# Four layers on one core: the last batch's normalisation by ScalarE in two passes, and the last pair's products evicted by VectorE

## The chip, the cores and the metric

The kernel runs on one core of a Trainium2 chip. A time is the device time of one execution in microseconds (us). The kernel before was timed in three executions, and one more was taken with the hardware profiler. Times in the text that look like "at 906.20" are microseconds from the start of the profiled span.

The engines are named as the profile names them: PE (TensorE) multiplies matrices, DVE is VectorE, ACT is ScalarE, POOL is GpSimd, SP is SyncE, which issues most DMAs. Each engine works through its own list of instructions in order.

## The reference, cut to what matters

Four sublayers follow one another on eight batches of 512 tokens by 256 features, each with a residual and a layernorm. The last is a mixture of experts, and the change lies behind it:

```python
dispatch, combine = ...            # top 2 of 8 experts, capacity 160, in 2 groups of 2048 tokens
expert_in = jnp.einsum('gtec,gth->egch', dispatch, x)
h = jax.nn.relu(jnp.einsum('egch,ehf->egcf', expert_in, wi))
expert_out = jnp.einsum('egcf,efh->egch', h, wo)
y = jnp.einsum('gtec,egch->gth', combine, expert_out)
...
x = _layernorm(x + y, axis=-1)     # (x - mean) / sqrt(var + 1e-5) over the 256 features
```

## The kernel before, in words

Each batch is a tile of 128 partitions by `NC` = 4 chunks of 256 features. The sixteen steps (group, expert) are taken in an order in which the last pair of experts of group 1 are steps 14 and 15. An expert's two matrix products (`expert_in`, `expert_out`) leave its output in `eoT`. `combine(i)` turns three column blocks per pair back by PE into PSUM, multiplies each row by its gate while evicting it to a tile `eo`, and adds it to the rows of `y_d` in DRAM by an indirect DMA. `y_d` already holds the residual.

The last pair (`last`, steps 14 and 15) is not added in DRAM. Its three `eo` blocks stay on the chip, and the rest of the kernel runs on two tracks:

- `finish(b)` for the batches 4 to 7 of group 1 begins when the additions of step 13 have landed. It loads the batch from `y_d` into a tile `z` (SP), runs `layernorm`, and stores `z` to `out` (SP). `layernorm(..., on_act=True)` takes per chunk `bn_stats` and `bn_aggr` on DVE (lines 360, 361), then one small DVE instruction for variance + eps (`rsqrt`, tile `ln_rs`), one POOL instruction for the power -1/2 (also `ln_rs`), one small DVE instruction for the shift (`ln_nb`), and four ACT instructions that normalise a chunk each, with a per-partition scale and bias.
- `fetch`, `sums` and `finish_last` treat the rows that the last pair touches. `fetch` gathers them from `y_d` (`tail_y`), `sums` adds up on PE what the last pair brings each row (line 1674; the block of step 14 first, the two of step 15 after it, into three PSUM banks), and `finish_last` adds this on DVE, normalises three blocks, and scatters them into `out` with three indirect DMAs from POOL (`put`, line 1702). These rows must overwrite what the batches' stores wrote, so the first scatter waits for all stores of `out`.

The order of the instructions on each engine comes from a planner in the file. `op(engine, cost, t, fn, ...)` looks for the first free slot of its engine at or after the planned time `t`, books it there, and queues the call. `flush` issues the calls in order of planned time. An instruction that is planned earlier is therefore ahead of a later one on its engine, whatever the chip does. Instructions on `DVS` and `POOL` also book a shared slot list, "port". The stages are Python generators, and `interleave` resumes the one whose time comes first; a stage that resumes early books its slots before the others.

Due times set the order here. All four `finish` stages begin at one planned time, which is called T here, and queue their loads in the order 4, 5, 6, 7. They resume at the `landing` that the plan supposes, and book their whole layernorm at that moment:

```python
landing = t + (9.0 if g == 0 else 4.0 + 2.9 * (b - B // G))   # T + 4.0, 6.9, 9.8, 12.7
```

`tail["stored"]` is the planned time at which the stores have landed; `finish_last` books its scatters from there.

Of the kernel before, what the change touches and what calls it, by code (L numbers as in the profile page):

```python
# [11 lines left out]
F32 = mybir.dt.float32  # L12
F32R = mybir.dt.float32r
I32 = mybir.dt.int32
AF = mybir.ActivationFunctionType
ALU = mybir.AluOpType
# [4 lines left out]
P = 128  # L21
B, S, D = 8, 512, 256
NC = S // P
# [5 lines left out]
G = 2  # L29
# [9 lines left out]
LN_EPS = 1e-5  # L39
# [42 lines left out]
def tile_layers(ctx: ExitStack, tc: tile.TileContext, ins, out, at):  # L82
# [52 lines left out]
    ACT, DVE, POOL, SP, GELU, EXP, DVS, POOLD = range(8)  # L135
# [5 lines left out]
    V, A, GP, T = nc.vector, nc.scalar, nc.gpsimd, nc.tensor  # L141
# [3 lines left out]
    XB, TB, EX, B8 = 4, 3, 3, 2  # L145
    EW = 3

    class Plan:
        now = 0.0
        slow = 0.0  # L150
        t = 0.0
# [14 lines left out]
    def give(tag, t, n=1):  # L166
        Plan.free[tag] += [t] * n

    def take(tag, n=1):

        times = sorted(Plan.free[tag])
        assert len(times) >= n, tag
        Plan.free[tag] = times[n:]
        return times[n - 1]

    def op(engine, cost, t, fn, *args, use=None, drop=None, bank=None, **kw):


        if engine in (GELU, EXP):
            cost += 0.0 if engine == Plan.loaded else TABLE  # L180
            engine, Plan.loaded = ACT, engine
        users = [engine]
        if engine in (DVS, POOL):
            users.append("port")
        engine = users[0] = {DVS: DVE, POOLD: POOL}.get(engine, engine)
        t = t + HOP
        if use is not None:
            t = max(t, take(use) + HOP)
        if engine != SP:
            length = max(cost - OVERLAP[engine], 0.05)  # L190
            found = False
            while not found:
                found = True
                for user in users:
                    for a, b in Plan.busy[user]:
                        if t + length <= a:
                            break
                        if b > t:
                            t, found = b, False
            for user in users:  # L200
                bisect.insort(Plan.busy[user], (t, t + length))
                while Plan.busy[user][0][1] < Plan.t - 30.0:
                    Plan.busy[user].pop(0)
        Plan.count += 1
        heapq.heappush(Plan.events, (t, Plan.count, lambda: fn(*args, **kw)))  # L205
        t += cost
        if drop is not None:
            give(drop, t)
        if bank is not None:
            release(bank, t)  # L210
        return t
# [5 lines left out]
    def pe(cost):  # L217


        start = max(Plan.now, Plan.t)  # L220
        if start - Plan.now > 1.5:
            Plan.slow = start + (1.5 if start - Plan.now < 3.0 else 8.0)
        cost += min(max(Plan.slow - start, 0.0) / 2, cost)
        Plan.now = Plan.t = start + cost
        return Plan.now + PE_OUT
# [9 lines left out]
    def release(ps, t):  # L235
        Plan.banks[Plan.bank_of.pop(id(ps))[1]] = t

    def need(t, n=1):

        while True:  # L240
            r = max(t + HOP_PE, sorted(Plan.banks)[n - 1] + HOP if n else 0.0)
            yield "pe", r if r < HELD else Plan.t + 0.5
            if not n or sorted(Plan.banks)[n - 1] <= Plan.t + 1e-6:
                return
# [7 lines left out]
    def later(t):  # L252

        return "other", t
# [58 lines left out]
    def power(n):  # L313
        return {1: 0.56, 2: 0.7}.get(n, 1.02)

    def rsqrt(dst, src, scale, eps, t, bank=None):

        t = op(
            DVE if bank else DVS, 0.17, t, V.tensor_scalar, dst, src, scale, eps, ALU.mult, ALU.add,
            bank=bank,  # L320
        )
        return op(
            POOL, power(dst.shape[-1]), t,
            GP.tensor_tensor, dst, dst, mhalf.to_broadcast(list(dst.shape)), ALU.pow,
        )
# [26 lines left out]
    def layernorm(pool, dst, src, ts, on_act=False):  # L352


        st = pool.tile([P, NC, 6], F32, tag="ln_st", bufs=2, name="ln_st")
        mv = pool.tile([P, NC, 2], F32, tag="ln_mv", bufs=2, name="ln_mv")
        rs = pool.tile([P, NC], F32, tag="ln_rs", bufs=2, name="ln_rs")

        def stats(c):
            nc.vector.bn_stats(st[:, c, :], src[:, c, :])  # L360
            nc.vector.bn_aggr(mv[:, c, :], st[:, c, :])  # L361

        for c in range(NC):
            t = op(DVE, 0.61, ts[c], stats, c, use="ln" if c == 0 else None)
        ready = t = rsqrt(rs, mv[:, :, 1], 1.0, LN_EPS, t)
        if on_act:
            nb = pool.tile([P, NC], F32, tag="ln_nb", bufs=2, name="ln_nb")
            t = op(
                DVS, 0.16, t, V.scalar_tensor_tensor, nb, mv[:, :, 0], -1.0, rs, ALU.mult, ALU.mult
            )  # L370
        ends = []
        for c in range(NC):
            if on_act:
                e = op(
                    ACT, 0.58, t, A.activation, dst[:, c, :], src[:, c, :], AF.Identity,
                    bias=nb[:, c : c + 1], scale=rs[:, c : c + 1],
                )
            else:
                e = op(
                    DVS, 0.41, t, V.tensor_scalar, dst[:, c, :], src[:, c, :], mv[:, c, 0:1],  # L380
                    rs[:, c : c + 1], ALU.subtract, ALU.mult,
                )
            ends.append(e)
        give("ln", e)
        return mv, rs, ready, ends

    srcs, gates, logits = {}, {}, {}
# [181 lines left out]
    with ExitStack() as stages:  # L569
# [5 lines left out]
        wk = stages.enter_context(tc.tile_pool(name="wk", bufs=1))  # L575
# [869 lines left out]
        pools = {}  # L1445
# [131 lines left out]
        tail, stored = {}, []  # L1577

        def combine(i):


            g, e = order[i]
            last = i >= len(order) - 2
            pair, half = divmod(e, 2)
            n_in = added[g, pair]
            for j in ((0, 1), (1, 2))[half]:
                n_in[j] += 1
            for j, n in enumerate(COLS):
                if n_in[j] != (1, 2, 1)[j]:
                    continue  # L1590
                n_in[j] = -9
                col = pair * 3 + j
                yield from need(0.0)
                ps = bank("eo_tp")
                for m in range(NK):
                    T.transpose(  # L1596
                        ps[:n, m * P : (m + 1) * P], eoT[g, pair][:, m, j * P : j * P + n], ident
                    )
                eo = wk.tile([P, D], F32, tag="scm", bufs=SCM, name=f"eo_{g}_{col}")
                t = op(  # L1600
                    ACT, 0.47, pe(0.24), A.activation, eo[:n], ps[:n, :D], AF.Copy,
                    scale=gates[g][:n, col : col + 1], bank=ps, use="scm",
                )
                if last:
                    tail[j], done = eo, t
                    continue
                done = op(
                    POOLD, 1.87, max(t, Plan.landed), GP.indirect_dma_start,
                    out=y_d[g], in_=eo[:n], in_offset=None, compute_op=ALU.add,
                    out_offset=bass.IndirectOffsetOnAxis(ap=srcs[g][:n, col : col + 1], axis=0),  # L1610
                )
                Plan.landed = done + 2.9
                give("scm", Plan.landed)
            if max(n_in) < 0:
                give("xsT", Plan.now)
                give("eoT", Plan.now)
            yield later(done)
            return done + (0.0 if last else 2.9)
# [63 lines left out]
        def finish_last():  # L1682
# [46 lines left out]
            yield later(t)  # L1729
            return t + 3.0  # L1730

        def finish(b):

            g = b * G // B
            z = wk.tile([P, NC, D], F32, tag="x", bufs=XB, name=f"z_{b}")
            t = Plan.t
            dma(t, z, rows_of(y_d, b))
            landing = t + (9.0 if g == 0 else 4.0 + 2.9 * (b - B // G))
            yield later(landing)
            e = max(layernorm(wk, z, z, [landing] * NC, on_act=(g == 1))[3])  # L1740

            def store():
                stored.append(
                    nc.sync.dma_start(out=out[b].rearrange("(c p) d -> p c d", p=P), in_=z)
                )

            op(SP, 0.0, e, store)
            tail["stored"] = max(tail.get("stored", 0.0), e + 2.5)
            give("x", e + 4.0)
            yield later(e + 4.0)  # L1750
            return e + 2.5
# [4 lines left out]
        n = len(order)  # L1756
# [105 lines left out]
```

## Time and profile before

| What | Value |
|---|---|
| device time, median of 3 (range) | 930.57 us (930.12 to 933.92) |
| device time of the profiled execution | 931.42 us |
| its span | 929.6 us, 18769 instructions |
| mean granted PE clock | 0.982 |
| busy PE / DVE / ACT / POOL | 881.7 / 607.9 / 453.0 / 397.2 us |
| loads of the batches 4 to 7, issued | 896.8 to 898.6 |
| stores of these batches, issued | 906.7, 909.9, 913.1, 916.3 |
| three last scatters, begun on POOL | 919.98, 921.33, 923.66 |

Over nearly the whole span PE is busy. The rows below concern the last 35 us only: from the start of the `finish` loads to the end. In a timeline row the columns are start, duration, engine, line, operation, out<-in, shapes, count, and in brackets the idle time of the engine before it with what ended it. Line 205 is the planner's call, so that tiles and not lines tell the operations apart.

### The profile page before, as it was taken

To read this page: it belongs to the slowest core of one execution; us is meant where nothing else is said; L and a number is where in the kernel's file an instruction comes from. 1 tells how busy PE (TensorE), PEld (TensorE's weight loads), DVE (VectorE), ACT (ScalarE), POOL (GpSimd) and SP (SyncE) were. 2 spreads that over 40 slices of the span, in tenths; PEclk is the share of its full clock that TensorE was granted. 3 is DMA by queue.
4 is the path that set the end of the run, shared out by engine and by line. 5 is a ranking of instruction groups with operands and counts; after the bars stand their busy time and mean duration, and the time that the engine had idled before them with its cause. 6 is when DMAs were issued, how large, how long until landed. Compare 5 with 4: busy or idle time off the path is not lost. (4 is left out here: it accounts for less than half of the span.)

```text
span 929.6 us, 18769 instructions
## 1 busy us (share of the span) xinstructions
PE 881.7 (95%) x7628; PEld 687.9 (74%) x7628; DVE 607.9 (65%) x1530; ACT 453.0 (49%) x866; POOL 397.2 (43%) x404
## 2 busy tenths in 40 slices
PE   7899999999999999999999999999999999999892
PEld 4777777777767677677767676786787889999781
DVE  3945367669777847877887778578678654621223
ACT  2327356537652684486287535838536343122223
POOL 2425542744453263445434542732653332362233
PEclk9999999999999999999999999999999999999795
DMA  7030000001000100010020001050143356168742
GB/s 212 12 114 1 1 2 1 2 24 46 2 1 24 47 2 2 23 47 1 1 69 2 1 2 46 2 182 1 46 126 115 108 185 196 24 191 290 241 116 105
DMA packets 49894, 60.69 MB, mean 65 GB/s; under 512 B 5680, under 2 KB 44784, under 8 KB 49808
## 3 DMA queue, kind: packets, MB, share of 16 engines
q1 hardware_dynamic: 45952, 53.92, 17.4%
q0 software_dynamic: 3856, 5.57, 3.1%
q8 instruction: 60, 0.98, 0.4%
q14 instruction: 26, 0.21, 0.1%
HBM read 43.76 MB, written 15.73 MB: 64 GB/s over the span
## 5 line engine op out<-in xcount | busy, mean ns | idle before, releaser
L1167 PE MATMUL pr_ps<-prT,fT 128*128 128x257 f32 x512 | 117.4, 381 | 0.2 <-DVE f_ss L205 0.2
L1167 PEld LDWEIGHTS pr_ps<-prT,fT 128*128 128x128 f32 x512 | 95.2, 190 | 14.7 <-DVE f_ss L205 0.5
L205 POOL TENSOR_TENSOR fsq<-fsq,fsf 128x512 f32<-128x512 f32 x56 | 72.2, 1288 | 37.5 <-ACT fsf L205 35.3
L1530 PE MATMUL wi_ps<-xsT,wi 128*128 128x160 f32 x512 | 78.2, 308 | 0.1
L1559 PE MATMUL wo_ps<-e_hT,wo 128*128 128x160 f32 x512 | 74.5, 301 | 0.0
L1530 PEld LDWEIGHTS wi_ps<-xsT,wi 128*128 128x128 f32 x512 | 73.3, 196 | 1.3 <-ACT xsT L205 0.6
L205 DVE TENSOR_TENSOR hm<-hs,cst 128x512 f32<-128x512 f32 x96 | 60.2, 675 | 19.6 <-PE hs L1306 19.1
L1559 PEld LDWEIGHTS wo_ps<-e_hT,wo 128*128 128x128 f32 x512 | 70.8, 190 | 1.8 <-issue 1.5
L205 DVE TENSOR_TENSOR scm<-sc,cst 128x512 f32<-128x512 f32 x96 | 60.8, 679 | 15.4 <-PE sc L955 15.4
L205 ACT ACTIVATE e_hT<-wi_ps 128x480 f32<-128x480 f32 (+1 forms) x48 | 25.3, 526 | 87.4 <-PE wi_ps L1530 87.4
L205 POOL TENSOR_TENSOR ln_rs<-ln_rs,mhalf 128x4 f32<-128x4 f32 x32 | 33.3, 1040 | 80.7 <-DVE ln_rs L205 80.7
L205 POOL DMA_INDIRECT y_d<-eo,srci x21 | 32.8, 1561 | 71.4 <-ACT eo L205 35.7
L205 POOL TENSOR_TENSOR scm<-scm,cst 128x512 f32<-128x512 f32 x32 | 41.2, 1289 | 49.7 <-ACT scm L205 49.7
L205 DVE STREAM_TRANSPOSE hT<-pad 128x512 f32<-128x512 f32 x64 | 59.3, 959 | 3.5 <-ACT pad L205 3.0
L905 PE MATMUL qk_ps<-xT,wqkv 128*128 128x512 f32 x128 | 60.6, 617 | 1.0 <-ACT xT L205 1.0
L1247 PE MATMUL qk_ps<-l1T,x2T 128*128 128x512 f32 x128 | 61.5, 603 | 0.0
L205 POOL TENSOR_TENSOR hm<-hm,cst 128x512 f32<-128x512 f32 x32 | 41.1, 1284 | 33.5 <-ACT hm L205 33.5
L1138 PE MATMUL fc_ps<-x1T_l,fcT 128*128 128x512 f32 x128 | 53.8, 420 | 0.6 <-DVE x1T_l L205 0.5
L205 POOL TENSOR_SCALAR pad<-pad,lamv 128x128 f32<-128x128 f32 x32 | 12.0, 374 | 97.9 <-DVE pad L205 97.9
L1138 PE MATMUL fc_ps<-x1T_h,fcT 128*128 128x512 f32 x128 | 50.2, 392 | 0.0
L205 ACT ACTIVATE x<-x,ln_nb,ln_rs 128x256 f32<-128x256 f32 x64 | 33.2, 589 | 33.7 <-DVE ln_nb L205 33.5
L205 DVE COPY eoT<-wo_ps 128x320 f32<-128x320 f32 x16 | 7.8, 488 | 62.4 <-PE wo_ps L1559 62.4
(257 smaller groups left out, 2015.9 us busy)
## 6 DMA issues: line engine op xcount, KB each, us to landing
wi<-in_L_ffn_wi SPq DMA_DIRECT2D x13, 1024.0 KB, 6.8
wo<-in_L_ffn_wo SPq DMA_DIRECT2D x13, 1024.0 KB, 7.9
x<-in_L_attn_x SPq DMA_DIRECT2D x8, 512.0 KB, 3.9
x_d<-a SPq DMA_DIRECT2D x8, 512.0 KB, 3.0
y_d<-a SPq DMA_DIRECT2D x8, 512.0 KB, 4.2
z<-y_d SPq DMA_DIRECT2D x8, 512.0 KB, 6.1
out<-z SPq DMA_DIRECT2D x8, 512.0 KB, 3.5
prepare<-in_L_ffn_W_fc SPq DMA_DIRECT2D x4, 256.0 KB, 9.2
```

The source lines that it names most:

```text
L205: heapq.heappush(Plan.events, (t, Plan.count, lambda: fn(*args, **kw)))
L905: T.matmul(ps, wqkv[:, k, which * D + m * P : which * D + (m + 1) * P], xT[:, k, :], start=(k == 0), stop=(k == NK - 1),)
L1138: T.matmul(ps, fcT[:, k, f * P : (f + 1) * P], x[:, k, :], start=(k == 0 and x is low), stop=(k == NK - 1 and x is high),)
L1167: T.matmul(acc[:, : D + 1], hT[:, f, c * P : (c + 1) * P], prT[:, f, :], start=(f == 0), stop=(f == NF - 1),)
L1247: T.matmul(qk, x2T[:, k, cs], l1T[:, k, 0:2, :].rearrange("p a d -> p (a d)"), start=(k == 0), stop=(k == NK - 1),)
L1530: T.matmul(ps[:, f * CAP : (f + 1) * CAP], wi[:, k, (f3 + f) * P : (f3 + f + 1) * P], x[:, k, es], start=(k == 0), stop=(k == NK - 1),)
L1559: T.matmul(ps[:, m * CAP : (m + 1) * CAP], wo[:, f, m * P : (m + 1) * P], hT[:, f, :], start=(f == 0), stop=(f == NF - 1),)
```

## The change

There are four edits.

- `combine`: the three evictions of the last pair go from ACT (`activation`, Copy with the gate as scale) to DVE (`tensor_scalar`, multiplied by the gate). One belongs to step 14 and two to step 15.
- `layernorm_act`, for batch 7 alone: ACT copies each chunk into a scratch tile with the row sums accumulated, DVE scales the four sums by -1/256, ACT squares each chunk with this as bias and the sums accumulated, then come the same small DVE, POOL and DVE instructions, and four ACT instructions that normalise. DVE has no `bn_stats` for this batch.
- `finish`: the planned landing of batch 7 is T + 5.0 instead of T + 12.7; the loads themselves are issued as before.
- `tail["stored"]`: a store is planned to land 3.9 after its layernorm instead of 2.5.

```diff
@@ combine
-                t = op(
-                    ACT, 0.47, pe(0.24), A.activation, eo[:n], ps[:n, :D], AF.Copy,
-                    scale=gates[g][:n, col : col + 1], bank=ps, use="scm",
-                )
+                gate = gates[g][:n, col : col + 1]
+                if last:
+                    t = op(
+                        DVE, 0.42, pe(0.24), V.tensor_scalar, eo[:n], ps[:n, :D], gate, None,
+                        ALU.mult, bank=ps, use="scm",
+                    )
+                else:
+                    t = op(
+                        ACT, 0.47, pe(0.24), A.activation, eo[:n], ps[:n, :D], AF.Copy,
+                        scale=gate, bank=ps, use="scm",
+                    )
@@ new, beside finish
+        def layernorm_act(z, t):
+            sq = wk.tile([P, D], F32, tag="ex", bufs=EX, name="last_sq")
+            st = pools[0].tile([P, 3, NC], F32, tag="last_st", name="last_st")
+            total, dev, nb = (st[:, i] for i in range(3))
+            for c in range(NC):
+                t = op(
+                    ACT, 0.6, t, A.activation, sq, z[:, c, :], AF.Copy,
+                    accum_out=total[:, c : c + 1], use="ex" if c == 0 else None,
+                )
+            t = op(DVS, 0.16, t, V.tensor_scalar, total, total, -1.0 / D, None, ALU.mult)
+            for c in range(NC):
+                t = op(
+                    ACT, 0.6, t, A.activation, sq, z[:, c, :], AF.Square,
+                    bias=total[:, c : c + 1], accum_out=dev[:, c : c + 1],
+                    drop="ex" if c == NC - 1 else None,
+                )
+            t = rsqrt(dev, dev, 1.0 / D, LN_EPS, t)
+            t = op(DVS, 0.16, t, V.tensor_tensor, nb, total, dev, ALU.mult)
+            for c in range(NC):
+                t = op(
+                    ACT, 0.58, t, A.activation, z[:, c, :], z[:, c, :], AF.Identity,
+                    bias=nb[:, c : c + 1], scale=dev[:, c : c + 1],
+                )
+            yield later(t)
+            return t
@@ finish
-            landing = t + (9.0 if g == 0 else 4.0 + 2.9 * (b - B // G))
+            landing = t + (9.0 if g == 0 else 4.0 + 2.9 * (b - B // G) if b < B - 1 else 5.0)
             yield later(landing)
-            e = max(layernorm(wk, z, z, [landing] * NC, on_act=(g == 1))[3])
+            if b < B - 1:
+                e = max(layernorm(wk, z, z, [landing] * NC, on_act=(g == 1))[3])
+            else:
+                e = yield from layernorm_act(z, landing)
...
-            tail["stored"] = max(tail.get("stored", 0.0), e + 2.5)
+            tail["stored"] = max(tail.get("stored", 0.0), e + 3.9)
```

## The prediction

> **What bounds the kernel now.** I began with the page. PE is busy for 881.7 of 929.6 us, but the change touches nothing before step 14 of the experts, so only the end can move. The chain of waits, read from the last loads on, tells what that end is made of (start, duration, what):
>
> ```profile
> span 929.6 us, 18769 instructions
> ...
> 896.82 3.89 DMA z<-y_d
> ...
> 914.02 0.17 DVE ln_nb L205
> ...
> 914.22 0.60 ACT z L205
> ...
> 916.32 2.79 DMA out<-z
> ...
> 919.98 1.05 POOL out L1702
> ...
> 921.33 0.99 POOL out L1702
> ...
> 922.34 0.59 POOL tail_st L205
> ```
>
> Loads, four layernorms, batch 7's store, then the scatters. Between the loads and 914.02 the chain lies on DVE, so I read DVE's timeline; its rows for batch 5 and 6 show the period of one batch:
>
> ```profile
> 904.40 0.16 DVE L205 SCALAR_TENSOR_TENSOR ln_nb<-ln_mv,ln_rs 128x4 f32<-128x4 f32 x1 [0.29 <-POOL ln_rs L205]
> 904.48 0.42 DVE L360 BATCH_NORM_STATS2 ln_st<-z 128x6 f32<-128x256 f32 x1
> ...
> 907.56 0.16 DVE L205 SCALAR_TENSOR_TENSOR ln_nb<-ln_mv,ln_rs 128x4 f32<-128x4 f32 x1 [0.64 <-POOL ln_rs L205]
> ...
> 910.79 0.16 DVE L205 SCALAR_TENSOR_TENSOR ln_nb<-ln_mv,ln_rs 128x4 f32<-128x4 f32 x1 [0.64 <-POOL ln_rs L205]
> ```
>
> The period is 3.23 us (907.56 to 910.79): four statistics at 0.53 each and about 1.1 for the power on POOL. Batch 7 is the fourth in this row, and the change lifts it out. So on the face of it there are 3.2 us to win. Whether they are won hangs on when batch 7's data are there and who stands behind whoever waits for them. The instructions that load `z`, cut to the last two, and ACT's timeline:
>
> ```profile
> L205 SPq DMA_DIRECT2D z<-y_d x2: 505/511/517, 898.0 to 898.6; - x2
> DMA to landing us min/median/max: 6.5/7.0/7.6
> ```
>
> ```profile
> 904.60 2.07 ACT L205 ACTIVATE z<-z,ln_nb,ln_rs 128x256 f32<-128x256 f32 x4 [6.47 <-DVE ln_nb L205]
> 906.58 0.81 ACT L205 ACTIVATE eo<-eo_tp,sgate 128x256 f32<-128x256 f32 x2
> 907.76 2.08 ACT L205 ACTIVATE z<-z,ln_nb,ln_rs 128x256 f32<-128x256 f32 x4 [0.37 <-DVE ln_nb L205]
> ```
>
> The last load, batch 7's, is issued at 898.6 and lands 7.6 later, at 906.2. Batch 4's (896.82 + 3.9) landed at 900.7. ACT starts to normalise batch 4 at 904.60, before batch 7 has landed.
>
> **The order that the change makes.** I worked the slots out by hand with the rule of `op`, from T, when the `finish` stages begin (T is 896.8 on the chip). Planned times serve for the order only; every duration below is a row's. The stage of batch 7 now resumes at T + 5.0, before those of 5 and 6, and books everything at once. On ACT: its four Copies at 5.05, 5.70, 6.35, 7.00; then batch 4's normalise, booked earlier, at 7.80 to 9.24; its four Squares from 9.72; three of batch 5's normalise in the gap at 12.17; batch 7's normalise from 13.82; batch 5's fourth at 16.19; batch 6's from 16.67. On DVE: batch 4's statistics, the copy to `eoT`, one statistic of batch 5, batch 4's `ln_nb` at 7.59, the scaling of batch 7's sums at 7.67, and only then the other statistics of batch 5, `ln_rs` of 5, the two evictions of step 15, and the rest. Right behind the three additions of `finish_last` comes batch 6's `ln_nb`.
>
> So the plan believes in data at T + 5.0, and the chip has them at T + 9.4. ACT's head is a Copy that waits until 906.2, with batch 4's normalise behind it. DVE's scaling waits for the Copies, with three quarters of batch 5, and the evictions that PE waits for, behind it.
>
> **The sum, part by part.** Copies: the nearest row is the square with row sums of an earlier stage:
>
> ```profile
> L205 ACT ACTIVATE rms_sq<-a 128x256 f32<-128x256 f32 x4 | 1.7, 418 | 0.5 <-DVE a L205 0.4
> L205 ACT ACT_TABLE_LOAD x1 | 1.3, 1283 | 0.0
> ...
> L205 ACT ACTIVATION_READ_ACCUMULATOR rms_sq<-a 128x1 f32 x4 | 0.7, 187 | 0.0
> ```
>
> In its timeline four of these take 2.13 (637.50 to 639.63), 0.54 apart. Four Copies: 906.25 to 908.4. Bounds: a plain COPY of this size takes 372 (nearly 1 less over four), one with a pointer operand more (see below).
>
> Batch 4's normalise, 2.07: 908.3 to 910.35. It ended at 906.67 before, so its store slips 3.7; nobody waits for that.
>
> Squares: a bias pointer is added. The normalise with two pointers takes 588, the square without 418, so about 0.085 for one; 0.62 apart, 910.3 to 912.75.
>
> DVE meanwhile: scaling 908.45 to 908.6, three statistics (1.6) to 910.15, `ln_rs` of batch 5 to 910.35, two evictions. For these the nearest row is the addition from PSUM of `finish_last`, 417 ns each and 1.08 for three; I take 0.76 for two, to 911.05 (bounds 0.7 and 1.0). On ACT they took 0.81, so that move is worth nothing by itself; they end at 911.05 instead of 907.39 because of what stands ahead of them. The block of step 14 is evicted by DVE while DVE idles before 900.7; it costs nothing, since its matmuls are planned, and ran, from 904.20. Three evictions fewer on ACT free no time that anything uses.
>
> Power of batch 5 on POOL, 1.02: 910.5 to 911.5, its `ln_nb` to 911.7; two statistics of batch 6 to 912.7. `ln_rs` of batch 7 (waits for the Squares) to 912.95, power to 914.15, two more statistics of 6 beside it, `ln_nb` of 7 to 914.3, `ln_rs` of 6 to 914.5, additions 0 and 1 to 915.2. Addition 2 needs the last matmul. The row of `sums`:
>
> ```profile
> 907.08 5.68 PE L1674 MATMUL tail_ps<-eo,tail_same 128*128 128x256 f32 x12 [1.18 <-ACT eo L205]
> ```
>
> From 910.75 these end at 916.45, addition 2 at 916.9, batch 6's `ln_nb` behind it at 917.0. ACT is no sooner: Squares to 912.75, three of batch 5 to 914.15, batch 7's four 914.35 to 916.4, batch 5's fourth to 916.9. Two independent chains meet at 917.0, so a faster PE wins 0.1 here. Batch 6's normalise: 917.05 to 919.1.
>
> SP now issues the stores as 4, 7, 5, 6 at about 910.4, 916.45, 916.95, 919.15. Alone a store lands in 2.8 (three of the four); the other took 3.7. Behind two others I take 3.2, bounds 2.8 and 4.0: landed at 922.35. From landing to the first scatter the rows have 0.87 (919.11 to 919.98): 923.2. `finish_last` meanwhile: its period on DVE is 1.82 (rows 914.10 and 915.92), so its third power on POOL runs from 921.55 to 922.1 and is just hidden by the store.
>
> The last edit counts here: before, the third power (922.34) stood between the second and third scatter, and the third began 2.33 after the second. With stores planned 1.4 later the slots put all three powers ahead of the scatters, so the third follows the second in 1.35: a gain of 0.98, already on the path. Scatters at 923.2, 924.55, 925.9, against 919.98, 921.33, 923.66.
>
> Net at the last scatter: 925.9 - 923.66 = +2.2 us (3.2 later at the first scatter, 1.0 given back). What follows it, 5.94 us to the span's end, is unchanged. Against the profiled execution's own 931.42 that is 933.6; that execution lies 0.85 above the median of the runs, so I predict 930.57 + 2.2 = 932.8. The unknown costs move it by -1.0 to +0.4 (Copies), +-0.2 (evictions), -0.4 to +0.8 (store), together some -1.4 to +1.2.
>
> **A rule that speaks against the change.** In the page "ScalarE: Activation LUTs" of the Trainium skill, the section "Table sets: the hidden batching unit" names relu, copy, identity and abs as functions in every set and does not name Square; "What ACT_TABLE_LOAD costs" puts a switch at about 2.66 us. The rows above say otherwise for Square: in that stretch (594.5 to 641) there is one load, at its start and for the exponential, then exponentials, and the four squares follow with no load. The last table loaded in the kernel is again the exponential's (786.05). By the rows the Squares cost no switch, +2.2; by the rule one lies on ACT's chain, +4.9. I go with the rows.
>
> **The rivals.** *It works as planned.* If batch 7 lands near T + 5, or the wait hides in ACT's idle 6.47 us, no queue is held up: batch 6's normalise ends near its planned 915.3, its store near 918.2, scatters at 919.0, 920.4, 921.75, against 923.66: -1.9, so 928.7. For it: DVE does lose 3.2 us of work. Against it: four loads of 512 KB are issued within 2 us and land 3.9, 5.7, 6.5 and 7.6 after issue; nothing in the diff moves the fourth forward.
>
> *Batch 7 lands late: slower.* Before, it had 3.3 us to spare (906.2, first used at 909.51). Now ACT's head waits for it, and all that follows shifts one for one. The longest of the eight `z` loads took 9.8 from issue; from 898.6 that is 908.4, so +2.2 more: 935.0. It is past 0.5% (4.65 us) when the landing is after 908.6; a table switch with the forecast's landing would pass it too, at 935.5. Against it: the 9.8 belongs to the first group, under another load.
>
> *It doesn't matter.* A Copy with row sums as fast as the plain one, and stores that don't hinder one another: about +0.8, 931.4.
>
> **How the numbers follow.** Forecast (stalled heads, +0.8 to +3.4, alone 931.4 to 934.0) 0.78; as planned 0.08; late landing or a switch 0.09; doesn't matter 0.05. Within 0.5% is about what a measurement of this kernel can tell from no change. The forecast, the third rival and the first (-1.9) all lie within it, and of the second about half: faster 0.02, same 0.91, slower 0.07. The range takes the forecast's unknown costs, the third rival, and half the way to the two outer ones: 930.0 to 934.8.
>
> **What would show it.** Right: ACT idle up to the landing of the last `z` load, first Copy about 906.2; batch 4's normalise after it, near 908.3; an idle DVE of nearly 4 us ended by ACT; `sums`' last group starting near 910.8; store order 4, 7, 5, 6; first scatter near 923 and the three 1.35 apart. Wrong: a first Copy before 905, a table load after 896, or batch 6's normalise well before 917.

## The result and the profile after

The changed kernel takes 933.30 us (median of 21 executions, 932.11 to 936.38); the kernel before 931.17 (21 executions, 929.18 to 933.92). The ratio is 1.0026, interval 1.0018 to 1.0033: slower by 2.4 us, or 1.7 to 3.1. The forecast was +2.2 us.

The changed kernel's profiled execution has a span of 930.4 us and a device time of 932.25. The end of this kernel begins when the additions of step 13 have landed, and that moment differs from execution to execution: the first `z` load was issued at 896.82 in the profile before and at 894.84 in this one. Spans of single executions therefore can't be set against each other to a microsecond. What can is the time from the first `z` load to the last scatter: 26.84 us before (923.66 - 896.82), 29.66 after (924.50 - 894.84). The end itself has grown by 2.82. Below, this is called the tail.

The chain of waits after, over the same stretch as before (start, duration, what):

```profile
897.01 8.31 DMA z<-y_d
905.32 0.02 issue
905.34 0.52 ACT last_sq L205 x2
...
907.50 0.17 DVE last_st L205
907.67 0.34 DVE ln_st L360
...
909.62 1.02 POOL ln_rs L205
...
912.11 1.02 POOL last_st L205
...
915.91 1.98 ACT z L205 x4
...
917.90 3.09 DMA out<-z
...
921.86 1.05 POOL out L1709
...
924.50 0.90 POOL out L1709
```

Before, the chain left the loads with the first of them (3.89 us, batch 4) and went along DVE. Now it leaves with the last (8.31 us, batch 7), crosses ACT's Copies, and only then comes to batch 5's statistics on DVE. The timelines of the two engines show the two queues standing still. ACT:

```profile
905.34 0.42 ACT L205 ACTIVATE last_sq<-z 128x256 f32<-128x256 f32 x1 [9.08 <-DMA z<-y_d]
...
907.38 2.06 ACT L205 ACTIVATE z<-z,ln_nb,ln_rs 128x256 f32<-128x256 f32 x4
909.34 0.49 ACT L205 ACTIVATE last_sq<-z,last_st 128x256 f32<-128x256 f32 x1
...
911.73 1.57 ACT L205 ACTIVATE z<-z,ln_nb,ln_rs 128x256 f32<-128x256 f32 x3
913.34 2.07 ACT L205 ACTIVATE z<-z,last_st 128x256 f32<-128x256 f32 x4
915.32 2.55 ACT L205 ACTIVATE z<-z,ln_nb,ln_rs 128x256 f32<-128x256 f32 x5
```

DVE:

```profile
902.92 0.13 DVE L205 SCALAR_TENSOR_TENSOR ln_nb<-ln_mv,ln_rs 128x4 f32<-128x4 f32 x1
907.50 0.17 DVE L205 TENSOR_SCALAR last_st<-last_st 128x4 f32<-128x4 f32 x1 [4.45 <-ACT last_sq L205]
907.58 0.42 DVE L360 BATCH_NORM_STATS2 ln_st<-z 128x6 f32<-128x256 f32 x1
...
909.42 0.88 DVE L205 TENSOR_SCALAR eo<-eo_tp,sgate 128x256 f32<-128x256 f32 x2
...
914.55 0.41 DVE L205 TENSOR_TENSOR tail_y<-tail_y,tail_ps 64x256 f32<-64x256 f32 x1 [0.51 <-PE tail_ps L1681]
914.89 0.15 DVE L205 SCALAR_TENSOR_TENSOR ln_nb<-ln_mv,ln_rs 128x4 f32<-128x4 f32 x1
```

Batch 4's shift row (`ln_nb`) is ready at 903.05, yet its normalise begins at 907.38: it stands behind four Copies that wait for another batch. Batch 5's data are there and have one statistic done, yet the other three begin at 907.58, after a DVE that idled 4.45 us for the scaling of batch 7's sums. From 905.34 on ACT is never free for 0.15 us, and batch 6's normalise comes when everything else on ACT is done: the last row holds batch 5's fourth chunk and batch 6's four. POOL's timeline shows what is given back, the even distance of the three scatters:

```profile
919.48 0.53 POOL L205 TENSOR_TENSOR tail_st<-tail_st,mhalf 64x1 f32<-64x1 f32 x1 [1.24 <-DVE tail_st L1703]
...
921.86 1.05 POOL L1709 DMA_INDIRECT out<-tail_y,tail_row  x1 [1.81 <-DMA out<-z]
...
923.21 0.99 POOL L1709 DMA_INDIRECT out<-tail_y,tail_row  x1 [0.18 <-issue]
...
924.50 0.90 POOL L1709 DMA_INDIRECT out<-tail_y,tail_row  x1 [0.19 <-issue]
```

The third power is ahead of all scatters; from the first scatter to the third it is 2.64 us, where it was 3.68.

### The profile page after: what moved, and what is told of

It reads as the page before. It is cut to its first block, busy times and chain, and to the rows that moved or that the text cites. A ratio compares the mean times of both kernels' runs of the same rounds, so it can differ in the third digit from the quotient of the medians.

```text
span 930.4 us, 18775 instructions
## 1 busy us (share of the span) xinstructions
PE 878.5 (94%) x7628; PEld 686.4 (74%) x7628; DVE 606.4 (65%) x1526; ACT 455.5 (49%) x879; POOL 395.9 (43%) x404
```

## The experiments

The theory: two heads of queues wait for batch 7's landing because the plan has it too early; this costs more than the even scatters give back. Two questions lie beside it: is the early due time the whole fault, and which of the four edits is worth what?

**Batch 7 planned where it lands.**

```diff
-            landing = ... if b < B - 1 else 5.0)
+            landing = ... if b < B - 1 else 9.5)
```

> The changed kernel with batch 7 planned to land at T + 9.5 (where its load does land) instead of T + 5.0. Measure beside the time: start of the third scatter after the first z load's issue, 26.84 us in the kernel before, 29.66 in the changed one. Theory A (the early due time is the whole fault; without the stalled heads the change pays): third scatter near 25, time 1 to 2 us under before. Theory B (a stall, but also a chain of two passes on ACT that is too long behind a landing at 9.4): Copies between batch 4's and 5's normalise, squares from about 14.9 after the first load, batch 7's store near 21.1 against 19.5 before, third scatter near 28, time +1.1 to +1.4 us over before, about 1 under the changed kernel. I expect B.

Measured: ratio 1.0024 (1.0011 to 1.0037), so +2.2 us (1.0 to 3.4); tail 28.31 (922.87 - 894.56), 1.47 above before and 1.35 below the changed kernel. The long waits at the heads of both queues are gone. From ACT's timeline:

```profile
902.64 2.07 ACT L205 ACTIVATE z<-z,ln_nb,ln_rs 128x256 f32<-128x256 f32 x4 [6.71 <-DVE ln_nb L205]
904.82 0.42 ACT L205 ACTIVATE last_sq<-z 128x256 f32<-128x256 f32 x1
...
909.05 0.51 ACT L205 ACTIVATE last_sq<-z,last_st 128x256 f32<-128x256 f32 x1 [0.24 <-DVE last_st L205]
...
913.08 2.07 ACT L205 ACTIVATE z<-z,last_st 128x256 f32<-128x256 f32 x4
915.06 0.59 ACT L205 ACTIVATE z<-z,ln_nb,ln_rs 128x256 f32<-128x256 f32 x1
```

And from the chain:

```profile
915.67 3.69 DMA out<-z
```

Batch 4 is normalised at 902.64, but from batch 7's first Copy (904.82) to the end of its normalise (915.15) it is 10.3 us. The passes share ACT with two other batches, whose chunks take 3.6 of it (four of batch 5 and three of batch 6). Its data lie ready 10.2 after the first load (the fourth load is issued at 896.6 and lands 8.2 later). Before, batch 7 took 6.8 from its first statistic on DVE (909.51) to the end of its normalise (914.22 + 2.07). Theory A is ruled out: without the stalls the kernel is still slower than before. Theory B fits, but not in every part. Two Copies stand before batch 5's normalise and two behind it, and the last store is batch 6's, not batch 7's: its fourth chunk stands behind batch 7's normalise. The first scatter starts 2.51 us later after the first load than before; 1.61 of that is the later last store and 0.90 its longer landing (3.69 against 2.79), whose cause is open. What the due time alone costs is shown by the tail of one execution only (1.35). The timed runs don't tell this version from the changed kernel (ratios 1.0024 and 1.0026), though the interval leaves room for the tail's value.

**The longer store alone, in the kernel before.**

```diff
-            tail["stored"] = max(tail.get("stored", 0.0), e + 2.5)
+            tail["stored"] = max(tail.get("stored", 0.0), e + 3.9)
```

> The kernel before with one edit: a store is planned to land 3.9 after its layernorm instead of 2.5. The plan then puts the third power of the last rows ahead of the scatters on POOL. Theory A (this is worth the gap between second and third scatter): that gap falls from 2.33 to 1.35 us, time -1.0 us. Rival (the third block's normalise or the stores set the end): third scatter where it was, 0. I expect A.

Measured: ratio 0.9990 (0.9980 to 1.0000), so -0.9 us; tail 25.84 (921.80 - 895.96), 1.00 below before. The scatters on POOL start 1.36 and 1.29 apart:

```profile
919.15 1.05 POOL L1702 DMA_INDIRECT out<-tail_y,tail_row  x1 [0.78 <-issue]
...
920.51 0.99 POOL L1702 DMA_INDIRECT out<-tail_y,tail_row  x1 [0.18 <-issue]
...
921.80 0.90 POOL L1702 DMA_INDIRECT out<-tail_y,tail_row  x1 [0.19 <-issue]
```

A holds, to the tenth in the tail; the interval of the time just touches no change. In the changed kernel the same edit turned out to do nothing: with 2.5 put back there, the planner gives the same instructions in the same order on all five engines, because the third power is then planned 1.75 ahead of the first scatter in any case. The even scatters came from the new order, not from the 3.9.

**The evictions alone, in the kernel before.** The `combine` part of the diff and nothing else.

> The kernel before with one edit: the last pair's three evictions on DVE. Theory A (they fit into DVE's wait for batch 5's power): batch 7's shift row and the third scatter where they were, 0 +- 0.3 us. Rival (0.76 us of DVE work on the chain of four layernorms): +0.8 us. I expect A; the plan leaves the third power between the second and third scatter, so no gain from that.

Measured: ratio 1.0000 (0.9988 to 1.0012); tail 26.83 (925.90 - 899.07). A holds: moved by themselves the evictions cost nothing and bring nothing. The two of step 15 take 0.88 on DVE, against 0.81 on ACT and the 0.76 of my sum. The shift rows of the batches 6 and 7 show how they fit in:

```profile
913.57 0.16 DVE L205 SCALAR_TENSOR_TENSOR ln_nb<-ln_mv,ln_rs 128x4 f32<-128x4 f32 x1
...
916.27 0.16 DVE L205 SCALAR_TENSOR_TENSOR ln_nb<-ln_mv,ln_rs 128x4 f32<-128x4 f32 x1 [0.18 <-POOL ln_rs L205]
```

They take the place of one statistic of batch 6 in the wait for batch 5's power, so that batch 6's shift row comes 3.76 after batch 5's (909.81) instead of 3.23. Two statistics of batch 7 then stand in the wait for batch 6's power, and its shift row comes 2.70 later instead of 3.23. The sum is the same.

**Batch 7's load first.**

```diff
-                for bs in ([0, 1], [2, 3], [4], [5], [6], [7])
+                for bs in ([0, 1], [2, 3], [7], [4], [5], [6])
```

> The changed kernel with batch 7's load issued first (then 4, 5, 6); the order of all instructions on DVE, ACT and POOL is unchanged. Theory A (ACT's and DVE's heads wait for batch 7's landing): first Copy near 4.0 after the first load instead of 10.5, DVE's idle before the scaling gone, batch 4's statistics 2 us later, third scatter near 27.2: about 2.3 us under the changed kernel, near the kernel before (-0.1 +- 0.5). Rival (the extra ACT work or the new order sets the end whatever lands when): third scatter stays near 29.7, time +2.2 over before. I expect A.

Measured: ratio 1.0007 (0.9997 to 1.0017), so +0.7 us (-0.3 to +1.6); tail 28.65 (924.91 - 896.26). With not one compute instruction moved, this is 1.8 us under the changed kernel by the ratios, 1.0 by the medians and 1.0 in the tail, where 2.5 were expected. ACT's first Copy starts 3.9 after the first load, so the landing was what the heads waited for. DVE's timeline tells where the rest went:

```profile
903.33 0.43 DVE L360 BATCH_NORM_STATS2 ln_st<-z 128x6 f32<-128x256 f32 x1 [6.59 <-DMA z<-y_d]
...
906.99 0.16 DVE L205 SCALAR_TENSOR_TENSOR ln_nb<-ln_mv,ln_rs 128x4 f32<-128x4 f32 x1 [0.29 <-POOL ln_rs L205]
907.06 0.16 DVE L205 TENSOR_SCALAR last_st<-last_st 128x4 f32<-128x4 f32 x1
...
915.97 0.41 DVE L205 TENSOR_TENSOR tail_y<-tail_y,tail_ps 64x256 f32<-64x256 f32 x1 [1.44 <-PE tail_ps L1681]
916.31 0.15 DVE L205 SCALAR_TENSOR_TENSOR ln_nb<-ln_mv,ln_rs 128x4 f32<-128x4 f32 x1
```

The 4.45 before the scaling are gone. But batch 4, now second, is there 7.1 after the first load: 3.2 later than in the changed kernel, where 2 were expected. Everything on DVE comes later with it, the copy to `eoT` included, so PE starts the last pair's transposes late. All of `sums` then takes 8.69 us at a granted clock of 0.51, and batch 6's shift row stands behind an addition that waits 1.44 for PE; ACT waits 0.76 for that row. One late head has become another. How often the clock was so low in the timed runs isn't on record.

**The scaling of the sums on ACT, so that DVE waits for nothing.**

```diff
-            t = op(DVS, 0.16, t, V.tensor_scalar, total, total, -1.0 / D, None, ALU.mult)
+            t = op(ACT, 0.25, t, A.activation, total, total, AF.Copy, scale=-1.0 / D)
```

> The changed kernel with the scaling of batch 7's row sums (128x4, by -1/256) on ACT itself, planned at 0.25, instead of DVE, so that DVE has nothing at its head that waits for batch 7's Copies; ACT's head still waits. DVE's statistics of batch 5 and the evictions of step 15 should move forward by some 4 us, and sums' last group with them. Theory A (ACT's own row of Copies, batch 4's normalise, squares, and the normalise of 5, 7 and 6 ends as late by itself): third scatter 29.4 to 30.2 after the first z load (29.66 in the changed kernel, 26.84 before), time within 0.5 us of the changed kernel's. Theory B (DVE's stall is what costs): third scatter 25 to 27, time 0 to 2 us under before. I expect A.

Measured: ratio 1.0027 (1.0018 to 1.0035), the changed kernel's own; tail 30.24 (926.75 - 896.51), at the upper end of what was expected; batch 7 landed 10.8 after the first load here, 0.3 later than in the changed kernel's profile. Two rows of DVE's timeline:

```profile
907.01 0.87 DVE L205 TENSOR_SCALAR eo<-eo_tp,sgate 128x256 f32<-128x256 f32 x2
...
914.11 0.17 DVE L205 TENSOR_SCALAR last_st<-last_st 128x4 f32<-128x4 f32 x1 [4.15 <-ACT last_sq L205]
```

The evictions come 10.5 after the first load instead of 14.6, and `sums` is done 14.0 after it instead of 19.7. It brings nothing: DVE waits 4.15 further on, for the squares, and ACT's last normalise ends 23.6 after the first load, against 23.0 in the changed kernel. From batch 7's first Copy on, ACT works without a gap here too. Its row of work behind the late landing is enough by itself. A holds; DVE's stall is real and not what decides.

**A version without the two passes.** The experiments point to what may pay: even scatters, and a layernorm chain on DVE that doesn't wait for POOL. In the kernel before, batch b's shift row waits 0.64 for the power, since only one statistic of the next batch is planned between. With the loads planned 2.3 apart two of them are. A third buffer for mean and variance, factor and shift goes with it (`give` hands it to the planner); the diff is shortened.

```diff
-        mv, rs, nb: bufs=2
+        mv, rs, nb: bufs=3
-            landing = t + (9.0 if g == 0 else 4.0 + 2.9 * (b - B // G))
+            if b == B // G:
+                give("ln", t)
+            landing = t + (9.0 if g == 0 else 4.0 + 2.3 * (b - B // G))
-            tail["stored"] = max(tail.get("stored", 0.0), e + 2.5)
+            tail["stored"] = max(tail.get("stored", 0.0), e + 3.9)
```

> A version that drops the two passes on ACT: the kernel before, with a store planned to land 3.9 after its layernorm, loads planned 2.3 apart instead of 2.9 (so that a batch's shift row stands behind two statistics of the next batch and no longer waits for POOL's power), and a third buffer for mean/variance, factor and shift. Theory A: the period of a batch on DVE falls from 3.23 to about 2.6 us for batches 6 and 7, batch 7's store 1.0 us sooner, the scatters 1.35 apart: third scatter near 24.8 after the first load, time -2.0 us. Rival (the loads of 6 and 7 land too late for that, or POOL's power is longer than two statistics): only the scatters' 1.0, third scatter near 25.9. I expect A.

Measured: ratio 0.9970 (0.9962 to 0.9979), so -2.8 us (2.0 to 3.5), 928.68 against 931.22; tail 25.22 (920.39 - 895.17), 1.62 below before. It is faster than both kernels. DVE's shift rows:

```profile
906.46 0.16 DVE L205 SCALAR_TENSOR_TENSOR ln_nb<-ln_mv,ln_rs 128x4 f32<-128x4 f32 x1
...
909.09 0.16 DVE L205 SCALAR_TENSOR_TENSOR ln_nb<-ln_mv,ln_rs 128x4 f32<-128x4 f32 x1
...
911.79 0.16 DVE L205 SCALAR_TENSOR_TENSOR ln_nb<-ln_mv,ln_rs 128x4 f32<-128x4 f32 x1 [0.17 <-POOL ln_rs L205]
```

The period is 2.63 and 2.70, where it was 3.23, and the waits for POOL are gone but for 0.17. In the tail 1.0 comes from the scatters and 0.6 from the chain, less than the 1.0 expected: batch 5's first statistic waited for its load to 7.6 after the first one. Why the times show more than the tail isn't settled by one profile; the third buffer serves every layernorm of the kernel, not only the last four, and was not measured by itself. The forecast of -2.0 lies on the interval's edge.

## Why the prediction was right, point by point

- *ACT's head waits for batch 7, batch 4's normalise behind it.* So it was: a first Copy at the landing, DVE idle 4.45 where "nearly 4" was forecast, stores in the order 4, 7, 5, 6.
- *The landing, 9.4 after the first load.* Mis-sized. It was 10.5 here, and between 10.0 and 10.8 for the fourth load in all six experiments; the 9.4 of the profile before was the shortest of all. I had taken one landing for a constant. ACT's first Copy is 1.1 later than in the sum; shorter steps further on give back half of that, so that the tail is 0.6 longer than the sum (29.66 against 925.9 - 896.82 = 29.08).
- *Copies 2.13, batch 4's normalise 2.07, squares 0.62 apart.* Copies from 905.34 to the normalise's start at 907.38 are 2.04, the normalise 2.06, the squares 0.63 apart. No table load came: the rows were right to weigh more than the rule. The +4.9 for a switch was too much in any case: the rows before show one at 786.05 between two ACTIVATEs 1.31 us apart (786.03 to 787.35), all but one of the kernel's others take as long, and the 2.66 shows in none of them. One switch on ACT's chain would have meant some +3.5, an estimate from these rows.

```profile
785.46 0.57 ACT L205 ACTIVATE e_hT<-wi_ps 128x480 f32<-128x480 f32 x1 [0.86 <-PE wi_ps L1530]
786.05 1.28 ACT L205 ACT_TABLE_LOAD   x1
787.35 0.23 ACT L205 ACTIVATE choose<-logits 128x32 f32<-128x32 f32 x1
```

- *Two independent chains that meet at batch 6's normalise.* Nearly. The last group of `sums` took 4.56 instead of 5.68, the shift row was ready at 915.04, and ACT reached it at 915.81. ACT's chain decides, by 0.8, and the experiment with the scaling on ACT shows that it does so alone. With the 5.68 of the forecast, by an estimate from these numbers, `sums` would have ended 1.1 later and DVE's chain would have decided, by 0.35.
- *Store behind two others 3.2.* It landed in 3.09 (917.90 to 920.99).
- *The last edit gives 0.98.* The size was right, its cause was not: in this kernel the edit does nothing, and the order that comes from lifting batch 7 out of DVE's row puts the power ahead. In the kernel before the same edit is worth 1.0.
- *The period of 3.23 as four statistics and the power.* The total was right, its parts were not: three statistics stand between one shift row and the power, and the fourth, of the next batch, runs beside the power, for which DVE then still waits 0.64. The sum did not rest on it; the version without the two passes does. The rows of DVE and POOL before:

```profile
909.51 0.42 DVE L360 BATCH_NORM_STATS2 ln_st<-z 128x6 f32<-128x256 f32 x1
...
909.75 1.01 POOL L205 TENSOR_TENSOR ln_rs<-ln_rs,mhalf 128x4 f32<-128x4 f32 x1 [2.22 <-DVE ln_rs L205]
```

- The sum: first scatter +3.2, given back 1.0, net +2.2. In the tail it is +3.9 (27.02 against 23.16) less 1.04, +2.8; by the medians +2.1, by the ratio +2.4. That the number came out closer in the timed runs than in the tail is partly luck: the sum stands on a landing that no other profile showed again. And a change of 0.5% was too coarse a limit for what can be told: 21 executions of each kernel gave an interval 0.15% wide.
- *As planned, -1.9:* failed at its first step, the landing. *Late landing, +4.4:* the landing did come later than in the profile before, by 1.1 and not by 2.2. *It doesn't matter, +0.8:* below the interval (1.7 to 3.1).

## What to carry to other kernels

In a list that an engine works through in order, a due time that is earlier than the data's landing doesn't start the work sooner; it moves the wait to the head of the queue, and everything behind pays, other engines too. Before moving work to an idle engine, ask for its data's landing and for the length of the new chain from that landing to the end: here it was 10.1 us from batch 7's first Copy to the end of its normalise (905.34 to 915.41), 3.6 of them other batches' work on ACT, where with the statistics on DVE, though batch 7 was fourth in its line, it took 6.8. And when one order change bundles several edits, run the small ones alone: a single number in the plan (2.5 to 3.9) was worth a microsecond in the kernel before, and nothing in the changed one.

## What I had not expected of the hardware

The same twelve matmuls of `sums` (the two blocks of step 15) took 5.68, 4.56 and 3.00 us. The windows of the stretch, for the kernel before, the changed one, the one with the scaling on ACT and the kernel before with the longer store (columns: stretch, length, busy time and count of PE, PEld, DVE, ACT, POOL, granted PE clock, DMA share, GB/s):

```profile
907.08:912.76 5.68, 5.68 (x12) 3.27 (x12) 4.11 (x18) 4.16 (x9) 1.45 (x2) 0.50 0.52 185
```

```profile
909.96:914.52 4.56, 4.56 (x12) 2.98 (x12) 3.53 (x15) 4.45 (x12) 2.66 (x3) 0.65 0.32 115
```

```profile
907.55:910.55 3.00, 3.00 (x12) 1.86 (x12) 2.00 (x8) 2.90 (x11) 0.60 (x1) 1.00 0.00 0
```

```profile
906.26:909.26 3.00, 3.00 (x12) 1.89 (x12) 2.29 (x10) 2.38 (x5) 0.78 (x2) 1.00 0.49 175
```

The clock does not follow the length of the idle time before them: PE had idled 1.18 us before the slow ones, 6.07 before the middle ones and 2.08 before the fast ones of the version with the scaling on ACT. The last window is the clearest: the longer store changes the order on POOL alone, PE has the same list of instructions as in the kernel before, and its gaps were almost the same (0.75 and 1.27 us, against 0.75 and 1.18), yet one execution had the full clock and the other half of it. Its row:

```profile
906.26 3.00 PE L1674 MATMUL tail_ps<-eo,tail_same 128*128 128x256 f32 x12 [1.27 <-ACT eo L205]
```

A row of PE behind a gap should be carried into a sum with both lengths; the Trainium skill's page "TensorE: Matmul & The Clock Gate", Part 1, has the clock decided in windows that run free of the program, which would make it a matter of phase; two executions that are alike on PE and differ in the clock agree with that, but no run here was made to show it.
